# Residual graph layers with norms on one core: weights of layers 0 to 2 without output means, norms from squares on ScalarE, another order in the gate bank

## The chip, the core and the metric

The kernel runs on one core of a Trainium2 chip. The metric is the device time of one execution in microseconds (us). The core's engines are TensorE (PE in the profile, its weight loads PEld), VectorE (DVE), ScalarE (ACT), GpSimd (POOL) and SyncE (SP), which here issues the DMAs. Each works through its own queue.

## What is computed

The input x has 64 batches of 256 nodes with 128 channels, in fp32; adj is a 256 x 256 matrix shared by all batches. Four layers follow one another, each of the form `x = layernorm(x + layer(x))`, the norm running over the 128 channels:

```python
# layer 0: powers of adj, each with weights of its own (adj is given twice)
y = sum over k of (adj^k x) @ weight_1[:, :, k]
# layer 1
y = adj @ (x @ weight) + bias
# layer 2
A = adj + I;  d = rowsum(A) ** -0.5;  y = (d A d) @ x @ W.T + b
# layer 3: five steps of a gated recurrence, h = x at first
av = concat(adj @ h, adj @ h);  u3 = h @ u3_w.T + u3_b
z = sigmoid(av @ w3_w.T + w3_b + u3)
r = sigmoid(av @ w4_w.T + w4_b + u3)
hv = tanh(av @ w5_w.T + w5_b + (r * h) @ u5_w.T + u5_b)
h = (1 - z) * h + z * hv
# the norm
(x - mean(x)) / sqrt(var(x) + 1e-5)
```

## The kernel before

**Groups.** Two batches make a group, 32 groups in all; up to eight are under way at once. A group's values are tiles of 128 partitions by 512 columns: four blocks (q) of 128, each 128 nodes by 128 channels in the natural layout, so that a norm is over a block's columns.

**The order is planned.** Each operation is recorded with its engine, an estimated cost, a lag, and the values that it reads and writes (`Plan.add`). `Plan.order` then places them one by one: of all that are ready, the one that can start first, and among equals the older group. PSUM banks (eight) and SBUF slots are handed out by the same plan. The instructions are issued in this order, so the order in each engine's queue is fixed when the kernel is built, from the estimates and not from what the chip does.

**Layers 0 to 2.** Layer 0 uses w0s, which holds the weights of x (with the identity added, which gives the residual), of adj x, and of the next two powers, each the sum of both weights. It is transposed on the way through `p`, `v` and `s0`. Layers 1 and 2 propagate y (`propagate`, a product in seven block products with sums made by GpSimd and DVE, see `seven`), multiply by the weights (w1s; w2T, a transposed copy of w2) into a bank `py`, and add yb, which is y plus the bias made on GpSimd (L711). `residual` (L481) adds py and yb on DVE.

**The norm.** `statistics` takes a tile s: on DVE four bn_stats (L461), four bn_aggr (L465), var + EPS (L467) and the negated mean (L468); on GpSimd (var + EPS) ^ -0.5 (L471) and mean times that (L472). `normalise` (L489) then makes y on ScalarE, one ACTIVATE a block, with the scale and the bias given per partition. All four norms of a group go this way, 128 in all.

**Layer 3.** hT is the transposed state, brought by way of DRAM (`turned`, `brought`; between the steps `packed`). Each step propagates h into m (mg in the profile), and one bank, pr, takes u3 hT and then w4 m; ACT reads r from it (L638). w34 is w3 less w4: added to the same bank it turns r's sum into z's. A second bank, ph, takes w5 m and u5 (r h) for hv. DVE makes rh, d, e and the new hT (L645).

**Start.** SP issues the loads of adj, of the first x, of the weights and biases, then the copies aTp and w0p that are spread over partitions in another way, and further loads of x. `pre` gives each a rank. The first two groups get their transposed x through TensorE; later ones through a transposition on DVE and DRAM.

Of the kernel before, what the change touches and what calls it, by code (L numbers as in the profile page):

```python
# [9 lines left out]
AF = mybir.ActivationFunctionType  # L10
OP = mybir.AluOpType
AX = mybir.AxisListType

P = 128
# [8 lines left out]
EPS = 1e-5  # L23
# [133 lines left out]
def kernel(  # L157
# [30 lines left out]
    nc = tc.nc  # L188
    B, N, C = x.shape
# [7 lines left out]
    def mm(o, lhsT, rhs, start, stop, shared=False):  # L197
        nc.tensor.matmul(o, lhsT, rhs, start=start, stop=stop, skip_group_check=shared)  # L198
# [7 lines left out]
    def constant(name, shape):  # L206
        v = Val("const", shape, name)
        v.tile = const.tile(shape, F32, name=name)
        return v
# [4 lines left out]
    def pre(rank, engine, cost, run, reads=(), writes=()):  # L214
        lag = {"SP": 2300, "PE": 260, "DVE": 260, "ACT": 130, "POOL": 100}[engine]
        plan.add(engine, cost, lag, rank, run, reads, writes)

    def load(rank, name, shape, src, keep=True):
        v = constant(name, shape) if keep else Val("w", shape, name)
        pre(rank, "SP", 450, lambda: nc.sync.dma_start(v.ap, src), [], [v])  # L220
        return v

    ident = const.tile([P, P], F32, name="ident")
    make_identity(nc, ident)
    half = const.tile([P, Q], F32, name="half")
# [18 lines left out]
    aT, a2T = constant("aT", [P, T, N]), constant("a2T", [P, T, N])  # L244
# [30 lines left out]
    w0s = constant("w0s", [P, 4, C])  # L275
# [6 lines left out]
    pre(-7, "DVE", 1300, w0_sums, [w0_raw], [w0s])  # L282


    w0p = constant("w0p", [P, 2, C])

    def permuted():
# [15 lines left out]
    ahat, anT = Val("w", [P, T, N], "ahat"), constant("anT", [P, T, N])  # L303
# [27 lines left out]
    def block_sums(rank, name, aTs):  # L331
# [3 lines left out]
        def run():  # L335
# [13 lines left out]

    w1s = load(1.3, "w1s", [P, C], w1)
    b1s = load(1.4, "b1s", [P, C], bass.AP(tensor=b1.tensor, offset=b1.offset, ap=[[0, P], [1, C]]))
    raw = {name: load(1.5, f"raw_{name}", [P, src.shape[1]], src, False)
           for name, src in (("w2", w2), ("w4", w4_w), ("w3", w3_w), ("w5", w5_w), ("u3", u3_w), ("u5", u5_w))}
    b2s = load(1.5, "b2s", [P, C], bass.AP(tensor=b2.tensor, offset=b2.offset, ap=[[0, P], [1, C]]))
    both = {name: Val("w", [P, C], f"both_{name}") for name in ("w4", "w3", "w5", "w34")}
    for name in ("w4", "w3", "w5"):
        pre(0.4, "DVE", 220, lambda o=both[name], i=raw[name]: nc.vector.tensor_add(
# [1 line left out]
    pre(0.4, "DVE", 220, lambda: nc.vector.tensor_sub(both["w34"].ap, both["w3"].ap, both["w4"].ap),  # L361
        [both["w3"], both["w4"]], [both["w34"]])

    def transposed(name, *parts_):
        ps, v = temp(f"p_{name}"), constant(name, [P, len(parts_) * P])

        def run():
            for i, src in enumerate(parts_):
                nc.tensor.transpose(ps.ap[:, i * P:(i + 1) * P], src.ap, ident)

        n = len(parts_) * P
        pre(0.4, "PE", len(parts_) * 110, run, parts_, [ps])
        pre(0.4, "ACT", act_cost(n), lambda: nc.scalar.copy(v.ap, ps.ap[:, :n]), [ps], [v])
        return [(v, v.ap[:, i * P:(i + 1) * P]) for i in range(len(parts_))]

    w2T, u3T = transposed("w2u3T", raw["w2"], raw["u3"])
    w4T, w34T, w5T, u5T = transposed("w435u5T", both["w4"], both["w34"], both["w5"], raw["u5"])

# [11 lines left out]
    def nat(v):  # L390
        return v.ap.rearrange("p (q c) -> p q c", c=C)
# [21 lines left out]
    class Group:  # L413
# [41 lines left out]
        def statistics(self, tag, s):  # L455
            st, mv, ve, rs, nm = (self.val(k, n + tag) for k, n in (
                ("st", "st"), ("mv", "mv"), ("ve", "ve"), ("rs", "rs"), ("ve", "nm")))

            def stats():
                for q in range(self.q):  # L460
                    nc.vector.bn_stats(st.ap[:, q * 6:(q + 1) * 6], nat(s)[:, q, :])  # L461

            def aggr():
                for q in range(self.q):
                    nc.vector.bn_aggr(mv.ap[:, 2 * q:2 * q + 2], st.ap[:, q * 6:(q + 1) * 6])  # L465
                mean, var = (mv.ap.rearrange("p (q k) -> p k q", k=2)[:, k] for k in range(2))
                nc.vector.tensor_scalar(ve.ap, var, EPS, None, op0=OP.add)  # L467
                nc.vector.tensor_scalar(nm.ap, mean, -1.0, None, op0=OP.mult)  # L468

            def scales():  # L470
                nc.gpsimd.tensor_tensor(rs.ap, ve.ap, half[:, :self.q], op=OP.pow)  # L471
                nc.gpsimd.tensor_tensor(mv.ap[:, :self.q], nm.ap, rs.ap, op=OP.mult)  # L472

            self.dve(stats, [s], [st], 195 * self.q)
            self.dve(aggr, [st], [mv, ve, nm], 67 * self.q + 240)
            self.add("POOL", 1420, 100, scales, [ve, nm], [rs, mv])
            return mv, rs

        def residual(self, tag, ps, resid, left=lambda v: v.ap, right=lambda v: v.ap):
            s = self.val("w", "s" + tag)  # L480
# [152 lines left out]
        def product(self, ps, w, rhs, start, stop, shared=False):  # L633
            self.pe(pe_cost(self.width), lambda: mm(ps.ap, w[1], rhs.ap, start, stop, shared), [rhs, w[0]], [ps])

        def gate_(self, name, ps, func, bias):
            t = self.val("w", name)
            self.act(lambda: nc.scalar.activation(t.ap, ps.ap, func, bias=bias[1], scale=1.0),  # L638
                     [ps, bias[0]], [t],
                     act_cost(self.width) + 100)  # L640
            return t
# [6 lines left out]
        def record(self):  # L648
# [7 lines left out]
            else:  # L656
# [9 lines left out]
                def run():  # L666
                    f = far.ap.rearrange("(k j) (r b n) -> b (j r) k n", k=4, r=4, b=self.nb)
                    for b in range(self.nb):
                        nc.sync.dma_start(xT.ap.rearrange("p (b k n) -> b p k n", b=self.nb, k=4)[b], f[b])
# [3 lines left out]
            v, s0 = self.val("w", "v"), self.val("w", "s0")  # L673
            py = []
# [16 lines left out]
            for t in range(T):  # L691
# [9 lines left out]

                self.pe(pe_cost(self.nb * C, T), second, [v, aT], [py[t]])
                self.act(summed, [py[t]], [s0], act_cost(self.nb * C))
            y = self.normalise("0", s0, *self.statistics("0", s0))


            for tag, ats, w, bias in (("1", aT, (w1s, w1s.ap), b1s), ("2", anT, w2T, b2s)):
                yb = self.val("w", "yb" + tag)

                def biased(yb=yb, y=y, bias=bias):  # L710
                    nc.gpsimd.tensor_tensor(nat(yb), nat(y), bias.ap[:, None, :].to_broadcast([P, self.q, C]),  # L711
                                            op=OP.add)

                self.add("POOL", 40 + 625 * self.nb, 100, biased, [y, bias], [yb])
                m = self.propagate(tag, y, ats)
                py = self.val("bank", "py" + tag)

                def weight(py=py, m=m, w=w):
                    for q in range(self.q):
                        mm(py.ap[:, q * P:(q + 1) * P], m.ap[:, q * P:(q + 1) * P], w[1], True, True)  # L720

                self.pe(pe_cost(P, self.q), weight, [m, w[0]], [py])
                y = self.normalise(tag, *self.residual(tag, py, yb))


            h = y
            hT = self.brought("hT", self.turned("h", h, "p (q k j) -> p q k j", "p (k q i) -> p q k i"))
            ats, ins = aT, None
            for s in range(STEPS):
                m = self.propagate(f"g{s}", h, ats, ins, True)  # L730
                pr = self.val("bank", f"pr{s}")
                self.product(pr, u3T, hT, True, False)
                self.product(pr, w4T, m, False, True)
                r = self.gate_(f"r{s}", pr, AF.Sigmoid, rb)
                rh = self.tensor(f"rh{s}", OP.mult, r, hT)
                ph = self.val("bank", f"ph{s}")
                self.product(ph, w5T, m, True, False)
                self.product(pr, w34T, m, False, True, shared=True)
                z = self.gate_(f"z{s}", pr, AF.Sigmoid, zb)
                self.product(ph, u5T, rh, False, True)  # L740
                hv = self.gate_(f"hv{s}", ph, AF.Tanh, hb)

                d = self.tensor(f"d{s}", OP.subtract, hv, hT)
                e = self.tensor(f"e{s}", OP.mult, z, d)
                if s < STEPS - 1:
                    hT = self.tensor(f"hT{s}", OP.add, hT, e)
                    h, ats, ins = self.packed(f"h{s}", hT), aTp, pairs
            if self.start < B - END:
                hT = self.tensor("hT", OP.add, hT, e)
# [3 lines left out]
            else:  # L753
                hT = self.tensor("hT", OP.add, hT, e, lambda v: v.ap.rearrange("p (k q i) -> p q k i", k=4, q=self.q),
                                 lambda v: v.ap.rearrange("p (q k i) -> p q k i", k=4, q=self.q))
# [23 lines left out]
    with tc.manual_schedule():  # L779
        for op in plan.order():  # L780
            for v in op.vals:
                if v.tile is None:
                    pool = {"bank": psum_b, "dram1": dram, "dram2": dram}.get(v.kind, sbuf)
                    full = SHAPES.get(v.kind, v.shape)
                    t = pool.tile(full, F32, tag=f"{v.kind}{v.slot}", name=v.name)
                    if v.shape != full:
# [3 lines left out]
                        t = t[:, :n]  # L790
                        if len(v.shape) == 3:
                            t = t.rearrange("p (a b) -> p a b", b=v.shape[2])
# [32 lines left out]
```

## Time and profile before

| | |
|---|---|
| time, median of three runs | 1392.04 us (1391.99 to 1392.26) |
| time of the profiled execution | 1391.42 us |
| mean granted TensorE clock | 0.993 |
| chain that ended last | PE 82%, DVE 13%, issue 2%, ACT 2%, DMA 1%, SPq 1% |
| DMA | 134.45 MB, 97 GB/s |
| r, z and hv on ACT | 160 each, 685 ns |
| rh, d, e, hT on DVE | 160 each, 787, 766, 761 and 788 ns |
| bn_aggr; var + EPS; negated mean on DVE | 512 of 151 ns; 128 of 252; 128 of 168 |
| power; mean times scale on GpSimd | 128 of 1123 ns; 128 of 265 |

How to read it: a row of the page's groups names the line, the engine, the operation, the tiles that it writes and reads with their shapes, and how often it runs; then the busy time in us and the mean duration of one in ns; then how long the engine had been idle before such instructions, and which instruction ended most of that (the releaser). Instructions of one engine overlap in part, so that the busy time of a group can be less than its number times its mean. An fp32 product shows as two matmul records, each with a weight load. The chain that ended last is followed back from the end of the execution, at each step to what released it.

### The profile page before, as it was taken

How to read it: one execution, taken by the hardware profiler on the slowest of the kernel's cores; microseconds unless marked ns; L12 is line 12 of the kernel's file. 1: busy time of each engine (PE TensorE's matmuls, PEld its weight loads, DVE VectorE, ACT ScalarE, POOL GpSimd, SP SyncE). 2: the span in 40 equal slices, each digit the busy share in tenths (PEclk: the TensorE clock that was granted, in tenths of full speed). 3: DMA queues.
4: the chain of work that ended last, by engine and by line, in shares of the span. 5: the costliest groups of instructions: out<-in, count | busy, mean ns of one | idle time of the engine just before them, and what ended most of it. 6: DMA issues, size and time to landing. Idle time of an engine off the chain costs nothing.

```text
span 1389.6 us, 22166 instructions
## 1 busy us (share of the span) xinstructions
PE 1347.1 (97%) x6516; PEld 928.3 (67%) x6516; DVE 1114.0 (80%) x3288; ACT 691.1 (50%) x1638; POOL 754.7 (54%) x1089
## 2 busy tenths in 40 slices
PE   8999999999999999999999999999999999899996
PEld 7976656676666766666577775666766667665663
DVE  5678779788887798888778798788888777988776
ACT  3554445455454445545455554544555444554444
POOL 4776526475564474754267575636655435853332
PEclk9999999999999999999999999999999999999998
DMA  6112225333343342433433323343333332133232
GB/s 190 33 54 84 84 69 167 100 98 100 91 115 91 101 113 72 131 88 117 117 87 104 93 77 91 92 128 101 91 115 107 91 90 71 52 124 104 87 91 61
DMA packets 269672, 134.45 MB, mean 97 GB/s; under 512 B 176368, under 2 KB 241392, under 8 KB 269552
## 3 DMA queue, kind: packets, MB, share of 16 engines
q1 hardware_dynamic: 269552, 133.03, 33.0%
q8 instruction: 53, 0.87, 0.3%
q14 instruction: 67, 0.55, 0.1%
HBM read 67.05 MB, written 65.54 MB: 95 GB/s over the span
## 4 chain that ended last, share of the span: by engine, by line
PE 82%; DVE 13%; issue 2%; ACT 2%; DMA 1%; SPq 1%; DVEq 0%; POOL 0%; ACTq 0%; POOLq 0%
PE pr L198 27%; PE ph L198 18%; PE pmg L198 16%; PE py L198 13%; PE pm L198 6%; PE pmq L198 2%; DVE hT L645 2%; DVE d L645 2%; DVE e L645 2%; DVE st L461 1%; DVE s L481 1%; DMA x<-in_x_dram 1%; DVE rh L645 1%; ACT hv L638 1%; DVE th L620 1%
## 5 line engine op out<-in xcount | busy, mean ns | idle before, releaser
L198 PE MATMUL pr<-mg,w435u5T 128*128 128x512 f32 x640 | 325.0, 597 | 2.3 <-DVE mg L569 2.2
L471 POOL TENSOR_TENSOR rs<-ve,half 128x4 f32<-128x4 f32 x128 | 143.7, 1123 | 232.8 <-DVE nm L468 230.7
L531 POOL TENSOR_TENSOR tsg<-h 128x256 f32<-128x256 f32 x128 | 105.2, 822 | 253.5 <-DMA h<-dh 187.6
L489 ACT ACTIVATE y<-s,mv,rs 128x128 f32<-128x128 f32 x512 | 210.6, 483 | 44.1 <-POOL mv L472 42.7
L638 ACT ACTIVATE z<-pr,bsum 128x512 f32<-128x512 f32 x160 | 109.5, 685 | 127.2 <-PE pr L198 125.0
L645 DVE TENSOR_TENSOR rh<-r,hT 128x512 f32<-128x512 f32 x160 | 125.9, 787 | 53.7 <-ACT r L638 52.8
L198 PE MATMUL pr<-hT,w2u3T 128*128 128x512 f32 x320 | 163.4, 598 | 4.2 <-DVE hT L645 3.3
L645 DVE TENSOR_TENSOR d<-hv,hT 128x512 f32<-128x512 f32 x160 | 122.5, 766 | 55.0 <-ACT hv L638 54.2
L198 PE MATMUL ph<-rh,w435u5T 128*128 128x512 f32 x320 | 163.5, 596 | 2.0 <-DVE rh L645 1.9
L638 ACT ACTIVATE r<-pr,bsum 128x512 f32<-128x512 f32 x160 | 109.6, 685 | 109.4 <-PE pr L198 109.1
L198 PE MATMUL ph<-mg,w435u5T 128*128 128x512 f32 x320 | 163.6, 593 | 0.0
L198 PEld LDWEIGHTS pr<-mg,w435u5T 128*128 128x128 f32 x640 | 110.2, 191 | 76.9 <-issue 59.1
L638 ACT ACTIVATE hv<-ph,bsum 128x512 f32<-128x512 f32 x160 | 109.2, 685 | 48.5 <-PE ph L198 47.9
L645 DVE TENSOR_TENSOR hT<-hT,e 128x512 f32<-128x512 f32 x160 | 125.6, 788 | 1.4
L198 PEld LDWEIGHTS pmg<-aTp,h 128*128 128x128 f32 x512 | 88.6, 197 | 52.7 <-issue 38.3
L198 PEld LDWEIGHTS pmg<-s_aTp,tsg 128*128 128x128 f32 x768 | 101.8, 191 | 32.2 <-issue 26.1
L645 DVE TENSOR_TENSOR e<-z,d 128x512 f32<-128x512 f32 x160 | 121.4, 761 | 1.4
L461 DVE BATCH_NORM_STATS2 st<-s 128x6 f32<-128x128 f32 x512 | 110.5, 275 | 3.6 <-ACT s L699 3.0
L198 PE MATMUL pmg<-s_aTp,tsg 128*128 128x128 f32 x768 | 106.5, 275 | 0.2 <-POOL tsg L535 0.2
L581 ACT COPY mg<-pmg 128x128 f32<-128x128 f32 x160 | 42.3, 264 | 121.6 <-PE pmg L198 90.4
L198 PE MATMUL pmg<-aTp,h 128*128 128x128 f32 x512 | 98.7, 280 | 0.5 <-DVE mq L569 0.3
L198 PEld LDWEIGHTS ph<-mg,w435u5T 128*128 128x128 f32 x320 | 58.0, 192 | 57.4 <-issue 41.6
(159 smaller groups left out, 2686.6 us busy)
## 6 DMA issues: line engine op xcount, KB each, us to landing
dh<-th SPq DMA_DIRECT2D x160, 256.0 KB, 2.0
h<-dh SPq DMA_DIRECT2D x256, 128.0 KB, 2.5
x<-in_x_dram SPq DMA_DIRECT2D x32, 256.0 KB, 3.4
hT<-dh SPq DMA_DIRECT2D x128, 64.0 KB, 2.0
out_dram<-y SPq DMA_DIRECT2D x32, 256.0 KB, 2.4
dx<-tx SPq DMA_DIRECT2D x30, 256.0 KB, 2.6
xT<-dx SPq DMA_DIRECT2D x60, 128.0 KB, 2.6
dn<-tn SPq DMA_DIRECT2D x28, 256.0 KB, 2.0
```

Of the source, the lines that this page charges most:

```text
L198: nc.tensor.matmul(o, lhsT, rhs, start=start, stop=stop, skip_group_check=shared)
L461: nc.vector.bn_stats(st.ap[:, q * 6:(q + 1) * 6], nat(s)[:, q, :])
L471: nc.gpsimd.tensor_tensor(rs.ap, ve.ap, half[:, :self.q], op=OP.pow)
L481: self.dve(lambda: nc.vector.tensor_add(right(s), left(ps), right(resid)), [ps, resid], [s])
L489: nc.scalar.activation(nat(y)[:, q, :], nat(s)[:, q, :], AF.Identity, bias=mv.ap[:, q:q + 1], scale=rs.ap[:, q:q + 1])
L531: nc.gpsimd.tensor_tensor(ts.ap[:, :2 * P].rearrange("p (x c) -> p x c", x=2), ins(h)[:, 1], ins(h)[:, :, 0], op=OP.subtract)
L581: self.act(lambda: nc.scalar.copy(o(m, 0), o(ps, 0, False)), [ps], [m], act_cost(P), True)
L620: self.dve(lambda: nc.vector.transpose(turn.ap.rearrange("p (u j t) -> p u t j", t=T, j=32), src.ap.rearrange("p (u t i) -> p u t i", t=T, ...
L638: self.act(lambda: nc.scalar.activation(t.ap, ps.ap, func, bias=bias[1], scale=1.0), [ps, bias[0]], [t], act_cost(self.width) + 100)
L645: self.dve(lambda: nc.vector.tensor_tensor(out(t), way(a), way(b), op=op), [a, b], [t])
```

## The change

Weights and biases of layers 0 to 2 are centred: from every row of w0s, of w1, and of the two biases the mean over the output channels is taken off, on DVE, before first use; for w2 the transposition is replaced by a product with the identity less 1/128. The outputs of these layers then have mean zero over the channels, as y has. So their norms need the mean square alone: ScalarE squares each block with an accumulator output, GpSimd adds EPS and takes the power, and ScalarE multiplies by it. The norm of layer 3 stays as it was. In each step of layer 3, w4 m is now the first product in the bank pr, and u3 h the second. w1, b1 and b2 are loaded into one tile, wb, with b2 written after b1.

```diff
+    def centre(v, means):
+        nc.vector.reduce_sum(means.ap, v.ap, axis=AX.X)
+        nc.vector.tensor_scalar(means.ap, means.ap, -1.0 / C, None, op0=OP.mult)
+        nc.vector.tensor_tensor(v.ap, v.ap, means.ap[:, :, None].to_broadcast(v.ap.shape), op=OP.add)
+    w0m = constant("w0m", [P, 4])
+    pre(-7, "DVE", 1500, lambda: centre(w0s, w0m), [w0s], [w0s, w0m])
...
-    w1s = load(1.3, "w1s", [P, C], w1)
-    b1s = load(1.4, "b1s", [P, C], bass.AP(tensor=b1.tensor, offset=b1.offset, ap=[[0, P], [1, C]]))
+    wb, wbm = constant("wb", [P, 3, C]), constant("wbm", [P, 3])
+    pre(1.3, "SP", 450, lambda: nc.sync.dma_start(wb.ap[:, 0, :], w1), [], [wb])
+    for i, b in ((1, b1), (2, b2)):
+        pre(1.4, "SP", 450, lambda i=i, b=b: nc.sync.dma_start(
+            wb.ap[:, i, :], bass.AP(tensor=b.tensor, offset=b.offset, ap=[[0, P], [1, C]])), [wb], [wb])
+    pre(0.35, "DVE", 1100, lambda: centre(wb, wbm), [wb], [wb, wbm])
...
-    b2s = load(1.5, "b2s", [P, C], bass.AP(tensor=b2.tensor, offset=b2.offset, ap=[[0, P], [1, C]]))
...
+    less = constant("less", [P, P])
+    pre(0.4, "DVE", 200, lambda: nc.vector.tensor_scalar(less.ap, ident, -1.0 / C, None, op0=OP.add), [], [less])
...
-                nc.tensor.transpose(ps.ap[:, i * P:(i + 1) * P], src.ap, ident)
+                if src is raw["w2"]:
+                    mm(ps.ap[:, i * P:(i + 1) * P], src.ap, less.ap, True, True)
+                else:
+                    nc.tensor.transpose(ps.ap[:, i * P:(i + 1) * P], src.ap, ident)
...
+        def spread_of(self, tag, s):
+            y, ve, rs = self.val("w", "y" + tag), self.val("ve", "ve" + tag), self.val("rs", "rs" + tag)
+            def squares():
+                for q in range(self.q):
+                    nc.scalar.activation(nat(y)[:, q, :], nat(s)[:, q, :], AF.Square, scale=C ** -0.5,
+                                         accum_out=ve.ap[:, q:q + 1])
+            def scales():
+                nc.gpsimd.tensor_scalar(ve.ap, ve.ap, EPS, None, op0=OP.add)
+                nc.gpsimd.tensor_tensor(rs.ap, ve.ap, half[:, :self.q], op=OP.pow)
+            self.act(squares, [s], [y, ve], 400 * self.q)
+            self.add("POOL", 1330, 100, scales, [ve], [ve, rs])
+            return y, rs
+        def normalise_centred(self, tag, s):
+            y, rs = self.spread_of(tag, s)
+            def run():
+                for q in range(self.q):
+                    nc.scalar.mul(nat(y)[:, q, :], nat(s)[:, q, :], rs.ap[:, q:q + 1])
+            self.act(run, [s, rs], [y], 380 * self.q)
+            return y
+        def added(self, tag, ps, resid):
+            s = self.val("w", "s" + tag)
+            self.dve(lambda: nc.vector.tensor_add(s.ap, ps.ap, resid.ap), [ps, resid], [s])
+            return s
...
-            y = self.normalise("0", s0, *self.statistics("0", s0))
+            y = self.normalise_centred("0", s0)
...
-                y = self.normalise(tag, *self.residual(tag, py, yb))
+                y = self.normalise_centred(tag, self.added(tag, py, yb))
...
-                self.product(pr, u3T, hT, True, False)
-                self.product(pr, w4T, m, False, True)
+                self.product(pr, w4T, m, True, False)
+                self.product(pr, u3T, hT, False, True)
```

More of the change, by code (lines that the diff above doesn't have):

```diff
@@ L348 @@
     block_sums(0.7, "aTp", aTp)
-    w1s = load(1.3, "w1s", [P, C], w1)
-    b1s = load(1.4, "b1s", [P, C], bass.AP(tensor=b1.tensor, offset=b1.offset, ap=[[0, P], [1, C]]))
+    wb, wbm = constant("wb", [P, 3, C]), constant("wbm", [P, 3])
[4 more added lines that the diff above has]
+    pre(0.35, "DVE", 1100, lambda: centre(wb, wbm), [wb], [wb, wbm])
+    w1c, b1c, b2c = ((wb, wb.ap[:, i, :]) for i in range(3))
     raw = {name: load(1.5, f"raw_{name}", [P, src.shape[1]], src, False)
            for name, src in (("w2", w2), ("w4", w4_w), ("w3", w3_w), ("w5", w5_w), ("u3", u3_w), ("u5", u5_w))}
-    b2s = load(1.5, "b2s", [P, C], bass.AP(tensor=b2.tensor, offset=b2.offset, ap=[[0, P], [1, C]]))
     both = {name: Val("w", [P, C], f"both_{name}") for name in ("w4", "w3", "w5", "w34")}
@@ L368, in run @@
             for i, src in enumerate(parts_):
-                nc.tensor.transpose(ps.ap[:, i * P:(i + 1) * P], src.ap, ident)
+                if src is raw["w2"]:
+                    mm(ps.ap[:, i * P:(i + 1) * P], src.ap, less.ap, True, True)
+                else:
+                    nc.tensor.transpose(ps.ap[:, i * P:(i + 1) * P], src.ap, ident)
         n = len(parts_) * P
-        pre(0.4, "PE", len(parts_) * 110, run, parts_, [ps])
+        pre(0.4, "PE", len(parts_) * 110, run, [*parts_, less], [ps])
         pre(0.4, "ACT", act_cost(n), lambda: nc.scalar.copy(v.ap, ps.ap[:, :n]), [ps], [v])
@@ L634, in product, with gate_ @@
             self.pe(pe_cost(self.width), lambda: mm(ps.ap, w[1], rhs.ap, start, stop, shared), [rhs, w[0]], [ps])
-        def gate_(self, name, ps, func, bias):
-            t = self.val("w", name)
+        def gate_(self, name, ps, func, bias, kept=True):
+            t = self.val("w", name) if kept else ps
             self.act(lambda: nc.scalar.activation(t.ap, ps.ap, func, bias=bias[1], scale=1.0),
@@ L703, in record @@
                 self.act(summed, [py[t]], [s0], act_cost(self.nb * C))
-            y = self.normalise("0", s0, *self.statistics("0", s0))
-            for tag, ats, w, bias in (("1", aT, (w1s, w1s.ap), b1s), ("2", anT, w2T, b2s)):
+            y = self.normalise_centred("0", s0)
+            for tag, ats, w, bias in (("1", aT, w1c, b1c), ("2", anT, w2T, b2c)):
                 yb = self.val("w", "yb" + tag)
                 def biased(yb=yb, y=y, bias=bias):
-                    nc.gpsimd.tensor_tensor(nat(yb), nat(y), bias.ap[:, None, :].to_broadcast([P, self.q, C]),
+                    nc.gpsimd.tensor_tensor(nat(yb), nat(y), bias[1][:, None, :].to_broadcast([P, self.q, C]),
                                             op=OP.add)
-                self.add("POOL", 40 + 625 * self.nb, 100, biased, [y, bias], [yb])
+                self.add("POOL", 40 + 625 * self.nb, 100, biased, [y, bias[0]], [yb])
                 m = self.propagate(tag, y, ats)
```

## The prediction

> **What bounds the kernel now.** I read the page's shares first, then TensorE's waits, then the chain of waits around the worst stall, then the end of the span.
>
> ```profile
> span 1389.6 us, 22166 instructions
> PE 1347.1 (97%) x6516; PEld 928.3 (67%) x6516; DVE 1114.0 (80%) x3288; ACT 691.1 (50%) x1638; POOL 754.7 (54%) x1089
> ...
> L489 ACT ACTIVATE y<-s,mv,rs 128x128 f32<-128x128 f32 x512 | 210.6, 483 | 44.1 <-POOL mv L472 42.7
> ...
> L461 DVE BATCH_NORM_STATS2 st<-s 128x6 f32<-128x128 f32 x512 | 110.5, 275 | 3.6 <-ACT s L699 3.0
> ```
>
> A busy TensorE is not TensorE at its pace, so I count its work. In the chain, four records of a 512-wide product take 1.72 us, so a product (two records) costs 0.86; eight records 256 wide take 1.74 (0.435 a product); sixteen 128 wide take 1.81 (0.226). The groups hold 800, 396 and 2034 of these products and 56 transposes at about 0.11: 688 + 172 + 460 + 6 = 1326 us. The other 64 us of the span are: 5.8 idle in the first 40 us, 13.6 idle after 1370 us, 23.1 idle in between, and 21 in which records are drawn out. About 40 us lie in the long middle and can be won. Who causes them is in TensorE's waits from 40 to 1370 us (total, times, longest):
>
> ```profile
> PE pmg L198 <- DVE mg L565: 5.2, 8, 2.1
> PE pr L198 <- DVE hT L645: 3.3, 6, 1.2
> PE py L198 <- DVE m L569: 2.8, 2, 1.8
> PE pm L198 <- DVE m L565: 2.6, 2, 2.2
> ...
> PE pr L198 <- ACT hv L638: 0.7, 1, 0.7
> ```
>
> The whole list names 22.4 us; DVE is the releaser of 18.5, ACT of 1.8. The releasing instructions are products' combinations and gates, not the norms; but the norms stand before them in DVE's queue. The chain of waits at the stall of 1202 us shows it (start, us, piece):
>
> ```profile
> 1198.10 1.67 DVE hT L645
> 1199.77 0.78 DVE st L461 x4
> 1200.55 0.61 DVE tn L599
> 1201.16 0.17 DVE usg L559
> 1201.33 0.30 DVE mv L465 x4
> 1201.63 0.02 issue
> 1201.65 0.17 DVE ve L467
> 1201.82 0.07 DVE nm L468
> 1201.89 0.19 DVE wsg L562
> 1202.08 0.34 DVE m L569
> 1202.43 0.04 issue
> 1202.47 0.94 PE py L198 x6
> ```
>
> Of these 4.3 us before py, 1.3 are st, mv, ve and nm. The window from 1180 to 1240 us, with DVE busy 55.73 of 60, is TensorE's worst in the middle: 5.85 us idle.
>
> **What the Trainium skill says.** (1) "Perfetto Trace Analysis", section Identifying the Most-Contended Engine: matmul busy time is no good measure of headroom. The trace agrees: 1347 busy against 1326 of work. (2) "PSUM — Partial Sum Buffer", section Engine vs sequencer instructions: the queues of ScalarE, VectorE and GpSimd are strict first in, first out. The chain above agrees: m waits behind nm. (3) "ScalarE: Activation LUTs", section What ACT_TABLE_LOAD costs: 186 ns + 0.833 a column, 93 more for each per-partition pointer operand, and 93 overlap back to back. For 128 columns and two pointers that is 479 alone, 386 in a row; the trace has a mean of 483, and 210.6/512 = 411 in a row. No page prices the accumulator output of an ACTIVATE.
>
> **The change part by part.**
> *Statistics of layers 0 to 2 leave DVE.* There are 128 norms, of which 96 lose st, mv, ve and nm. The four groups are busy 110.5 + 46.7 + 32.2 + 21.5 = 210.9 us, 1.65 a norm, so 96 x 1.65 = 158 us go; DVE drops from 1114 to about 959 us (69%).
> *Squares come to ScalarE.* 96 x 4 = 384 ACTIVATEs with an accumulator. The trace shows none. Below: 0.29 each (the skill's price with one pointer, in a row), 113 us. Above: 0.41 plus some 0.2 for fetching the sum (an estimate: half an ACTIVATE), 234 us. I take 0.41, the measured neighbour: 158 us, ACT at 849 (61%). The normalising pass then carries one pointer fewer; worth 0 to 36 us (384 x 0.093, the skill's price); I take 0. The program as built has one table load on ACT, as before.
> *GpSimd* keeps two small operations a norm: an addition of EPS in place of nm x rs (0.265 each, 33.9/128). Near nothing; between -10 and +20 us on an engine with 635 us of idle time.
> *Latency of a norm.* Before: st 0.86, mv to nm 0.6, GpSimd 1.3, ACT 1.65. After: squares 1.65, GpSimd 1.3, ACT 1.65. No longer; hidden by other groups.
> *Gate bank.* Same two products. In TensorE's order, weighed with the durations above, a median of 15.3 us of work lies from u3 h's start to w4 m's start, and 1.7 us from w4 m's to u3 h's afterwards. A bank is held some 13 us less, 160 times; u3 h no longer stands in the queue ahead of its time waiting for hT (3.3 us of the list). Against it: r now comes one product, 0.86 us, later after m. Eight groups share TensorE, and a step of one needs 5 x 0.86 + 7 x 0.226 = 5.9 us of it, so a round takes some 47 us and 0.86 is hidden, except in the last group. Bounds -6 to +6 in the middle (twice the waits that name hT); I take 0, and +1 at the end.
> *Start.* The centring of w0s adds a reduction over 512 columns (deg's takes 0.69), a small scaling (0.17) and a 512-wide addition (0.79): 1.7 us; that of w1, b1, b2 1.4; less 0.2. The first product with w0s starts at 14.4, w0s is complete at 8.9: hidden. One transpose becomes a product: +0.1 us of TensorE. On SP no DMA is added, but the order moves: six bias loads (1.45 + 1.92 us of issue) and b1 go ahead of aTp, w0p and the third load of x, which started at 14.50 and moves to about 18.4; the fourth from 18.44 to about 18.9. The later loads of x follow at +0.4 to +3.5. TensorE lost 2.4 us to x before 27 us, and the chain runs through a load of x until 32.9, so this reaches it: +1 (0 to +3).
>
> **The sum.** What freeing DVE is worth in the 40 us has two ends. Low: DVE's share of named waits, 18.5/22.4, gives 33 us, and 14% of DVE's work goes: 4.6. High: all that st, mv, ve and nm hold of the whole chain of waits, 18.9 + 7.4 + 6.7 + 2.2 = 35 us by adding its pieces, times 96/128: 26. I take 14, a little under the middle, since the next releaser is often close behind. ScalarE's share of the waits (8% of 40 = 3.2 us for 691 busy) grows with 158 us more, and squares stand four in a row ahead of gates: +3. Net -14 + 3 + 1 + 1 = -9 against the span of 1389.6. The profiled execution took 1391.42 and the timed runs 1391.99 to 1392.26, so the span is some 2 us short of a time; the same -9 from 1392.0 gives **1383 us**.
>
> **Rivals.**
> *ScalarE takes DVE's place (slower).* Place: a square block ahead of r in ACT's queue. From the second gate product to the product with rh, TensorE's order holds a median of 3.26 us of other work, while r (0.69) and rh (0.79) need 1.5: slack 1.8. A block of four at 0.41 (1.65) just fits; at 0.6 (2.4, with the accumulator's fetch) it overruns by 0.6 to 0.9, and the order was planned with 0.4 each. If a third of the 96 blocks hit a gate at 0.9: +29, less 14, plus 2: +17, **1409**. It decides from about 0.5 us a square. For it: the accumulator is unpriced. Against it: ACT would still be 40% idle, and 1.8 of 22.4 us of waits name it.
> *More is freed than DVE's time.* Banks held 13 us less let the planner start other products earlier, and a queue at 69% instead of 80% waits far less than in proportion: the 26 us are reached and only the start's 1 is lost: **1367**. For it: the releasers' list; against it: no wait of the list names a bank clearly.
> *Hidden anyway.* TensorE is saturated and its waits move from one DVE instruction to the next (d, e and hT alone hold 70 us of the chain): low end 4.6 less the costs of 5: **1391**. That the work is not removed can be left out: the built program has 128 BNStats instructions in place of 512.
>
> **How the numbers follow.** Forecast 0.50 (1375 to 1390), more freed 0.20, hidden 0.13, ScalarE 0.17. The range 1366 to 1400 leaves out part of the second and most of the last. About 0.2% (2.8 us) is what can be told from no change: faster takes the forecast but 0.02, the second case, and 0.03 of the third: 0.71; same 0.08; slower 0.21, ScalarE and the rest of the hidden case.
>
> **What would show it.** Right: BATCH_NORM_STATS2 x128, DVE near 960 us, ACT near 850, TensorE's idle time between 40 and 1370 us down from 23 to some 13, DVE's part of its waits down most. Wrong: squares over 0.5 us in a row, or r, hv or usg of ACT at the head of TensorE's waits (ScalarE); a TensorE idle time in the middle still near 23 (hidden); more than 3 us lost before 40 us or after 1370.

## The result, and the profile after

The changed kernel takes 1368.28 us (median of four runs, 1367.05 to 1369.0) against 1392.15 before (its median with a fourth run): a ratio of 0.9827, with a 95% interval of 0.981 to 0.9844. It is 24 us faster. The prediction said 9, and its rival "more is freed" named 1367. The runs below show that neither had the reason: over six orders of each kernel the means lie 7.5 us apart, with an interval of about -1 to 16, and the rest of the 24 us goes with the order that the planner happened to make.

The page after, its shares and the rows of the norms:

```profile
span 1365.1 us, 21963 instructions
PE 1335.7 (98%) x6517; PEld 923.9 (68%) x6517; DVE 983.1 (72%) x2335; ACT 763.7 (56%) x2406; POOL 747.0 (55%) x1089
...
L521 ACT ACTIVATE y<-s,rs 128x128 f32<-128x128 f32 x384 | 122.2, 393 | 13.7 <-POOL rs L510 13.3
L505 ACT ACTIVATE y<-s 128x128 f32<-128x128 f32 x384 | 113.8, 302 | 25.5 <-DVE s L528 25.3
```

DVE lost 131 us and ScalarE gained 73. The statistics on DVE are down to layer 3's:

```profile
L505 ACT ACTIVATION_READ_ACCUMULATOR y<-s 128x1 f32 x384 | 73.5, 191 | 0.0
...
L481 DVE BATCH_NORM_STATS2 st<-s 128x6 f32<-128x128 f32 x128 | 27.5, 277 | 0.3
```

The accumulator has a second instruction for each square, 191 ns long. The timeline of ScalarE (start, length, instruction) shows that it opens no gap in a row: the squares start 0.29 to 0.31 us apart, and each fetch lies half under its own square and half under the next.

```profile
600.21 0.31 ACT L505 ACTIVATE y<-s 128x128 f32<-128x128 f32 x1 [0.24 <-DVE s L528]
600.42 0.19 ACT L505 ACTIVATION_READ_ACCUMULATOR y<-s 128x1 f32 x1
600.52 0.29 ACT L505 ACTIVATE y<-s 128x128 f32<-128x128 f32 x1
600.72 0.19 ACT L505 ACTIVATION_READ_ACCUMULATOR y<-s 128x1 f32 x1
600.81 0.29 ACT L505 ACTIVATE y<-s 128x128 f32<-128x128 f32 x1
```

So four squares follow one another in 1.18 us: 0.295 a square, the lowest of the prices that the prediction weighed. The scaling in a row takes 0.318 (122.2/384) in place of 0.411.

Where the 24.5 us of span went: TensorE's idle time between 40 and 1340 us fell from 23.1 to 9.65 (1300 less 1290.35 busy), that of the first 40 us rose from 5.8 to 6.8, that after 1340 us went from 13.6 to 13.0, and its busy time fell by 11.4. TensorE's waits from 40 to 1340 us, the first rows:

```profile
PE pmg L198 <- ACT usg L624: 2.1, 3, 1.0
PE py L198 <- DVE m L621: 1.1, 3, 0.4
PE pmg L198 <- ACT s L752: 0.9, 1, 0.9
PE pr L198 <- ACT r L691: 0.9, 2, 0.6
```

In this list DVE as releaser is down from 18.5 to 3.5 us, and ScalarE is up from 1.8 to 5.6. Idle times of 1 us and more before one matmul were five, together 9.2 us; now there is one, of 1.0. The window from 1180 to 1240 us, worst before with 5.85 idle, has 0.40:

```profile
1180.00:1240.00 60.00, 59.60 (x270) 37.34 (x269) 48.29 (x109) 32.46 (x93) 27.89 (x42) 1.00 0.38 115
```

In the chain that ended last, DVE's share went from 13% to 5% and TensorE's from 82% to 89%. The middle reads as the prediction had it, only stronger. Whether it is the change's doing is another question.

### The profile page after: what moved, and what is told of

The parts are those of the page before. It is cut to its first block, busy times and chain, and to the rows that moved or that the text cites. A ratio compares the mean times of both kernels' runs of the same rounds, so it can differ in the third digit from the quotient of the medians.

```text
span 1365.1 us, 21963 instructions
## 1 busy us (share of the span) xinstructions
PE 1335.7 (98%) x6517; PEld 923.9 (68%) x6517; DVE 983.1 (72%) x2335; ACT 763.7 (56%) x2406; POOL 747.0 (55%) x1089
## 4 chain that ended last, share of the span: by engine, by line
PE 89%; DVE 5%; DMA 2%; ACT 1%; issue 1%; POOL 1%; SPq 1%; ACTq 0%; POOLq 0%; DVEq 0%
PE pr L198 28%; PE ph L198 19%; PE pmg L198 18%; PE py L198 15%; PE pm L198 6%; PE pmq L198 3%; DMA x<-in_x_dram 1%; DVE hT L698 1%; DVE d L698 1%; DVE e L698 0%; DMA w_raw<-in_L_gnn_weight_dram 0%; DVE th L672 0%; DVE rh L698 0%; DVE st L481 0%; DMA wb<-in_L_gnn_b_dram 0%
## 5 line engine op out<-in xcount | busy, mean ns | idle before, releaser
L698 DVE TENSOR_TENSOR d<-hv,hT 128x512 f32<-128x512 f32 x160 | 118.1, 738 | 69.5 <-ACT hv L691 68.5
L198 PEld LDWEIGHTS pr<-mg,w435u5T 128*128 128x128 f32 x640 | 107.1, 191 | 56.2 <-issue 38.2
L521 ACT ACTIVATE y<-s,rs 128x128 f32<-128x128 f32 x384 | 122.2, 393 | 13.7 <-POOL rs L510 13.3
L505 ACT ACTIVATE y<-s 128x128 f32<-128x128 f32 x384 | 113.8, 302 | 25.5 <-DVE s L528 25.3
L621 DVE TENSOR_TENSOR mg<-pmg,usg 128x256 f32<-128x256 f32 x160 | 67.1, 419 | 62.8 <-PE pmg L198 59.5
L510 POOL TENSOR_TENSOR rs<-ve,half 128x4 f32<-128x4 f32 x96 | 101.9, 1062 | 8.0
L509 POOL TENSOR_SCALAR ve<-ve 128x4 f32<-128x4 f32 x96 | 24.5, 255 | 141.8 <-ACT y L505 141.8
```

What stands on the lines that cost most here:

```text
L505: nc.scalar.activation(nat(y)[:, q, :], nat(s)[:, q, :], AF.Square, scale=C ** -0.5, accum_out=ve.ap[:, q:q + 1])
L509: nc.gpsimd.tensor_scalar(ve.ap, ve.ap, EPS, None, op0=OP.add)
L521: nc.scalar.mul(nat(y)[:, q, :], nat(s)[:, q, :], rs.ap[:, q:q + 1])
L621: nc.vector.tensor_tensor(o(m, slice(1, 3)), o(ps, slice(1, 3), False), both, op=OP.add)
L698: self.dve(lambda: nc.vector.tensor_tensor(out(t), way(a), way(b), op=op), [a, b], [t])
```

## The experiments

Each runs on the same chip as runs of the kernel before, whose medians lay between 1390.98 and 1392.36 us. In the first four, theory A says that the norms' leaving DVE brings the gain, theory B that the gate bank's order does, theory C that both do.

**One edit at a time.** The first has the changed norms with the old order of the gate products, the second the new order with the old norms.

```diff
 # e1: the changed kernel
-                self.product(pr, w4T, m, True, False)
-                self.product(pr, u3T, hT, False, True)
+                self.product(pr, u3T, hT, True, False)
+                self.product(pr, w4T, m, False, True)
 # e2: the kernel before, with the two lines exchanged the other way
```

> The changed kernel with u3 h first in the gate bank again, as before; all else as changed. Theory A (the norms' leaving DVE brings the gain): 1370 to 1374 us, DVE near 983 us, TensorE idle between 40 and 1350 us near 11. Theory B (the gate bank's order brings it): 1384 to 1390. Theory C (each brings about half): 1378 to 1382.

> The kernel before with only the two gate products exchanged (w4 m, then u3 h); norms as before on DVE. Theory A: 1388 to 1393 us. Theory B: 1370 to 1376. Theory C: 1378 to 1384.

Norms only took 1378.37 us (ratio 0.9906, 0.9891 to 0.9921), 12.6 less than before; the gate order only 1381.79 (0.9937, 0.9919 to 0.9955), 9.2 less. By the letter that is theory C, and the two sum to 21.8, near the whole. It would have been a neat end.

**Is it the time for which the bank is held?** In the next, u3 h comes first again, but is recorded as reading m too, so that the bank is opened only then.

```diff
-                self.product(pr, w4T, m, True, False)
-                self.product(pr, u3T, hT, False, True)
+                self.pe(pe_cost(self.width), lambda pr=pr, hT=hT: mm(pr.ap, u3T[1], hT.ap, True, False),
+                        [hT, m, u3T[0]], [pr])
+                self.product(pr, w4T, m, False, True)
```

> The changed kernel with u3 h first in the gate bank, but recorded as waiting for m too, so that the bank is opened only when m is there. If the gain of the gate edit lies in the time that the bank is held and in where u3 h stands in TensorE's queue: as the changed kernel, 1366 to 1371 us. If it lies in which product comes first: as the kernel with u3 h first and early. If Theory A holds alone, it and both others lie within 4 us of each other.

It took 1384.06 us (0.995, 0.9934 to 0.9967). In TensorE's order the median of the work from one gate product's start to the other's is 1.7 us, as in the changed kernel, and yet it is 16 us slower: the account by the bank fails as it was put. By the order of the products it should have matched the kernel with u3 h early, and it is 6 us slower than that. So something else may move these times by several us.

**The work given back to DVE, and taken off again without touching any order.** The fourth kernel does the old statistics on DVE once more, for nobody. The fifth plans them in the same way but issues nothing for them, so that TensorE's, ScalarE's and GpSimd's order is the fourth's to the last instruction.

```diff
 # e4: the changed kernel; stats and aggr as before the change, into tiles of their own
         def normalise_centred(self, tag, s):
+            self.idle_statistics(tag, s)
 # e5: the same plan
-            self.dve(stats, [s], [st], 195 * self.q)
-            self.dve(aggr, [st], [mv, ve, nm], 67 * self.q + 240)
+            self.dve(lambda: None, [s], [st], 195 * self.q)
+            self.dve(lambda: None, [st], [mv, ve, nm], 67 * self.q + 240)
```

> The changed kernel with the old bn_stats, bn_aggr and the two small operations still done on DVE for the norms of layers 0 to 2, their results read by nobody (extra work, nothing left out): DVE gets back some 158 us of busy time, ScalarE keeps the squares. Theory A: 1386 to 1394 us, DVE near 1140 busy. Theory B: 1369 to 1374. Theory C: 1378 to 1384.

> As the changed kernel with the statistics kept on DVE, and planned with them, but they are not issued (they were extra work, so nothing is left out): TensorE's, ScalarE's and GpSimd's order is that of the kernel with statistics kept, instruction for instruction, and only DVE's queue is shorter. Theory Q (a shorter DVE queue itself releases TensorE): 1376 to 1386 us against 1407 with the statistics issued. Theory P (the order of the plan decides, the queue's length little): 1396 to 1407.

With the statistics kept: 1406.93 us (1.0116, 1.0096 to 1.0137), above every theory's figure. Without issuing them, in the same order: 1392.22 (1.0004, 0.9997 to 1.0011), outside theory Q's range and theory P's alike, between the two. The engines' shares, with the statistics and without:

```profile
PE 1354.1 (96%) x6517; PEld 931.8 (66%) x6517; DVE 1106.1 (79%) x3295; ACT 766.4 (55%) x2406; POOL 739.2 (53%) x1089
PE 1351.8 (97%) x6517; PEld 932.4 (67%) x6517; DVE 984.2 (71%) x2335; ACT 766.4 (55%) x2406; POOL 742.2 (53%) x1089
```

So 122 us less on DVE brought 14.7 us, 0.12 for each, with every order the same. (The two ran on different chips; each set against the kernel before on its own chip, they differ by 16 us, 0.13 for each.) In TensorE's waits from 40 to 1340 us, those that DVE ends fall from 19.4 to 9.2 us, and those that ScalarE ends stay (8.6 and 9.0). The first rows, with the statistics kept:

```profile
PE pmg L198 <- DVE mg L635: 11.1, 12, 3.3
PE pmg L198 <- ACT usg L642: 4.6, 8, 1.9
PE pm L198 <- DVE m L635: 2.3, 2, 1.3
```

The same view of the kernel that does not issue them:

```profile
PE pmg L198 <- DVE mg L635: 6.9, 9, 2.4
PE pmg L198 <- ACT usg L642: 4.6, 8, 1.9
```

But this kernel does exactly what the changed one does, on the same engines, and is 24 us slower than it. Only the plan differs: the order, and the buffers that it hands out.

**The same work in other orders.** The planner's estimate for a DVE operation has a factor of 1.06. Moving it by 0.5 to 2% changes no work, but the plan made from it is another: with the changed kernel at 1.06 and at 1.05, fewer than one in five of TensorE's 3286 places hold the same product.

```diff
 def dve_cost(elements):
-    return (elements / 0.96 + 75) * 1.06
+    return (elements / 0.96 + 75) * 1.05
 # the other kernels: 1.07, 1.055, 1.065, 1.04
```

> The kernel before with the planner's estimate for DVE operations lowered by 1% (factor 1.06 to 1.05): the same work in another order. It measures what a redrawn order alone is worth. Theory P: 4 to 15 us away from 1391, either way. Theory Q: within 4 us of 1391.

> The changed kernel with the planner's estimate for DVE operations lowered by 1%: the same work in another order. Theory P: 4 to 15 us away from 1368, more likely above, as a single good draw returns to the mean. Theory Q: within 4 us of 1368.

> The kernel before with the planner's DVE estimate raised by 1% (1.06 to 1.07): another draw of the order. 1380 to 1395 us if draws lie some 6 us apart as the first suggests.

> The changed kernel with the planner's DVE estimate raised by 1%: another draw. If 1368 is typical and 1387 was the odd one: 1363 to 1374 us. If 1368 was a lucky draw: 1376 to 1390.

> The kernel before, planner's DVE factor 1.055. If draws of before scatter about their mean so far: 1379 to 1393 us. If 1391 is typical of before: 1388 to 1393.

> The changed kernel, planner's DVE factor 1.055. Change worth 24 us: 1364 to 1372. Change worth 9 to 12, the rest the draw: anywhere from 1367 to 1388.

> The kernel before, planner's DVE factor 1.065: as for 1.055, 1379 to 1393 us.

> The changed kernel, planner's DVE factor 1.065: as for 1.055; change worth 24: 1364 to 1372, worth 9 to 12: 1367 to 1388 us.

> The kernel before, planner's DVE factor 1.04: 1379 to 1391 us, near 1384 by the mean of its draws.

> The changed kernel, planner's DVE factor 1.04. Change worth 24: 1364 to 1372; worth some 7, the rest the draw: 1367 to 1388, near 1377 by the mean of its draws.

| factor | before, us | TensorE idle 40 to 1340 us | changed, us | TensorE idle 40 to 1340 us |
|---|---|---|---|---|
| 1.06 (as given) | 1392.15 | 23.1 | 1368.28 | 9.7 |
| 1.05 | 1385.67 | 19.4 | 1387.18 | 21.1 |
| 1.07 | 1380.60 | 16.7 | 1375.24 | 14.4 |
| 1.055 | 1384.77 | 18.9 | 1370.92 | 11.3 |
| 1.065 | 1378.77 | 13.2 | 1385.13 | 17.3 |
| 1.04 | 1390.58 | 21.2 | 1380.91 | 13.4 |
| mean (standard deviation) | 1385.4 (5.3) | | 1377.9 (7.7) | |

The means differ by 7.5 us, with a standard error of 3.8 (the root of 5.3²/6 + 7.7²/6), so roughly -1 to 16 as a 95% interval: a gain is likely, but not shown beyond doubt. The kernel before, as given, is the slowest of its six; the changed one is the fastest of its six. Without these two, the five redraws have means of 1384.1 and 1379.9, only 4.2 apart. Of the ten expectations, those that took 24 us for the change's worth held in one of four (1.055), and three results lay outside every range given: 1387.18, 1375.24 and, narrowly, 1378.77. In the pairs of the same factor the difference runs from 24 us faster to 6 slower. The time goes with TensorE's idle time: from the order with the least to that with the most, 9.9 us more idle stand against 13.4 us of time before, 11.4 against 18.9 after.

What an unlucky order looks like, in the timeline of the changed kernel at 1.05 (three of its eight idle times over 1 us; in brackets the idle time and the releaser):

```profile
188.78 0.69 PE L198 MATMUL pmg<-s_aTp,h 128*128 128x128 f32 x2 [2.58 <-issue]
...
234.80 0.38 PE L198 MATMUL pmg<-aTp,h 128*128 128x128 f32 x1 [2.74 <-ACT usg L624]
...
1024.08 0.50 PE L198 MATMUL pmg<-s_aTp,h 128*128 128x128 f32 x2 [1.66 <-DVE mg L617]
```

Over the six orders of each kernel, such idle times are 30 before and 24 after. DVE releases 22 of the 30 before, but 10 of the 24 after, where ScalarE releases 11. By all waits in this stretch it is the same: those that DVE ends fall from a mean of 12.1 us to 5.8, and those that ScalarE ends rise from 3.9 to 6.6. The norms' move thus shows in who is waited for, in all orders together.

**The two prices, in the orders as given.** One kernel is that of before, in its own order, with the statistics of layers 0 to 2 left out on DVE. The other is the changed one, in its own order, with one 4-column square for the four of 128 columns.

```diff
 # e9: before, for layers 0 to 2
+            if tag != "3":
+                def stats():
+                    nc.vector.memset(st.ap, 0.0)
+                def aggr():
+                    nc.vector.memset(ve.ap, 1.0)
+                    nc.vector.memset(nm.ap, 0.0)
 # e10: changed
-                for q in range(self.q):
-                    nc.scalar.activation(nat(y)[:, q, :], nat(s)[:, q, :], AF.Square, scale=C ** -0.5,
-                                         accum_out=ve.ap[:, q:q + 1])
+                nc.scalar.activation(ve.ap, nat(s)[:, 0, :self.q], AF.Square, scale=C ** -0.5)
```

> The kernel before in its own order, with the statistics of layers 0 to 2 left out on DVE: three small memsets stand for bn_stats, bn_aggr and the two small operations, so the norms of these layers scale by 1 and nothing is centred (this part of the computation is left out). GpSimd's and ScalarE's work stays. If a shorter DVE queue is worth the same 14 to 15 us as in the other order: 1375 to 1380 us. If it depends on the order: 1380 to 1388, or under 1372.

> The changed kernel in its own order, with one 4-column square in place of the four 128-column squares with accumulator (the mean squares of layers 0 to 2 are left out, their norms scale by something else). What it gains over 1368 is what the squares cost there. The prediction's +3: 1364 to 1366 us. If squares cost nothing: 1367 to 1369. If they stand in the way of the gates: under 1360.

The shares without the statistics, and without the squares:

```profile
PE 1342.7 (98%) x6516; PEld 927.4 (67%) x6516; DVE 996.8 (72%) x2616; ACT 691.0 (50%) x1638; POOL 747.7 (54%) x1089
PE 1337.6 (98%) x6517; PEld 925.6 (68%) x6517; DVE 980.7 (72%) x2335; ACT 667.0 (49%) x1734; POOL 749.8 (55%) x1089
```

Without the statistics: 1379.22 us (0.9917, 0.9901 to 0.9934), 12.0 less than the 1391.23 of before beside it. DVE's busy time fell from 1114.0 to 996.8, since the memsets stay, so that is 0.10 us for each us of DVE; in the other order it was 0.12. Without the squares: 1368.34 us, against 1368.28 with them; ScalarE's busy time fell from 763.7 to 667.0. In this order, 97 us of ScalarE cost nothing that can be measured.

The first of these kernels also tests the chain of waits that the prediction read at 1202 us. TensorE's order is that of before, and the wait ahead of the same product is gone (before, then without the statistics):

```profile
1202.47 0.94 PE L198 MATMUL py<-w1s,m 128*128 128x128 f32 x6 [1.81 <-DVE m L569]
1189.20 1.09 PE L198 MATMUL py<-w1s,m 128*128 128x128 f32 x8
```

Of the other waits over 1 us, that of 2.07 falls to 1.04 and that of 1.18 to 0.48; those of 1.94 and 2.18 stay.

**Truer estimates.** The planner counts 400 ns for a square and 380 for a scaling; the profile after has 295 and 318.

```diff
-            self.act(squares, [s], [y, ve], 400 * self.q)
+            self.act(squares, [s], [y, ve], 300 * self.q)
-            self.act(run, [s, rs], [y], 380 * self.q)
+            self.act(run, [s, rs], [y], 320 * self.q)
```

> The changed kernel with the planner's costs of the squares and of the scaling on ScalarE set near what the profile after shows (a square 0.295 us in a row and a scaling 0.318: estimates 300 and 320 in place of 400 and 380). If true costs help the plan: 1362 to 1367 us. If any new order is a new draw: 1364 to 1380.

1364.32 us (0.98, 0.9785 to 0.9814), the fastest of all and 4 us below the changed kernel. It is worth keeping as a kernel. As a rule it shows nothing: it lies in both ranges, and one order that lies 4 us off, where orders scatter by 7.7, may be one more draw. Counted with the kernel that plans the statistics and does not issue them (1392.22), it gives eight orders of the changed work: their mean stays at 1378.0, and their standard deviation is 9.9.

## Why the prediction was wrong

**Which step failed.** The sum, by a term that it lacks. It set "-14 + 3 + 1 + 1 = -9 against the span of 1389.6", as if the rest of the order stayed as it was, and gave the redrawn order no term at all. The plan is made anew from end to end whenever an operation goes or comes; a change of 0.5 to 2% in one estimate, with no work changed, is worth up to 13 us before (1391 to 1379) and 19 us after (1368 to 1387). The 24 us divide, by the six orders of each, into 7.5 between the means, 6.7 by which the kernel before stood above its own mean, and 9.7 by which the changed one stands below its. The range of 1366 to 1400 held the time, but its ends came from other causes, and that the rival "more is freed" named a figure within 2 us is luck: the mean of the changed kernel's six orders is 1378.

**Freeing DVE, taken as -14.** About right where the order is held, though not by the sum that led to it. The 158 us were the busy times of four groups added up, but instructions of DVE overlap: the same statistics, issued or not, moved DVE's busy time by 122 us, and in the changed kernel it fell by 131. At 0.10 to 0.13 us for each us, found in two orders that were held fixed, these 131 us are worth 13 to 17. The low end, 4.6 by proportion, is too low there; the high end, 26 by the chain's pieces, was not reached. What the same load is worth once the plan is redrawn is not shown.

**ScalarE, taken as +3.** Nothing, where it was tried. The squares take 0.295 us and not 0.41, the fetch of the sum opens no gap between squares, and the scaling saves the 36 us that I had left at 0. So ScalarE gained 73 us where I had 158. The slower rival decided from 0.5 us a square and fell with that. Still, over the six orders ScalarE takes DVE's place as the releaser of 11 of 24 long waits, and the waits that it ends grow by 2.7 us. So in a redrawn plan the +3 may hold; no run priced the squares there.

**The gate bank, taken as 0.** Not settled. The new order of the two products alone took 1381.79 us, well inside the range that the kernel before covers by redrawing (1378.77 to 1392.15). Norms only, at 1378.37, lies inside the changed kernel's. That 12.6 and 9.2 add up to about the 24 is therefore no proof for either part. That the bank's shorter hold helps, the ground of the faster rival, is not borne out, nor is it refuted: with the bank held as short, the kernel with u3 h late took 1384.06, but that is one order too. A fixed order could not be used here, since this edit is itself a change of order.

**Start, +1, and end, +1.** The first 40 us have 1.0 more idle, as put. After 1340 us there is 0.6 less; the last group's later r did not show.

**The reading of the bottleneck.** Right for the order as given: its waits lie in DVE's queue, and the changed kernel won 13.5 of idle time in the middle and 11.4 of drawn-out work. The stall at 1202 us was indeed the statistics' to remove: in the same order, without them, it is gone. What the trace of one order could not show is that this was also that order's stall: another order of the same kernel (1.065) has 10 us less idle in the middle with all its norms on DVE.

What is left open: the change's own worth, within about -1 to 16 us, and how the 7.5 divides between the norms, for which the fixed orders say 12 or more, and the rest.

## What to carry to other kernels

Where a planner or a scheduler fixes the order, an edit is compared with one draw of the order against another. Redraw both sides several times (six of each left 3.8 us of standard error here), by a change in an estimate that touches no work, before the difference is put on the edit. To price a load by itself, keep the plan and issue nothing for it: then the other engines' order is the same, and the difference is the load's.

## What the runs showed of the hardware

An idle time on TensorE can be paid twice. The kernel before waits 2.07 us for mg, until 325.28 us. Its stretches of 1 us around that (length; busy time and instructions of PE, PEld, DVE, ACT and POOL; then the granted clock, the DMA share, GB/s):

```profile
324.00:325.00 1.00, 0.00 (x0) 0.00 (x0) 0.97 (x9) 0.00 (x0) 0.55 (x1) 1.00 0.61 236
325.00:326.00 1.00, 0.72 (x6) 0.72 (x7) 1.00 (x7) 0.22 (x1) 0.67 (x2) 1.00 0.07 27
326.00:327.00 1.00, 1.00 (x8) 1.00 (x7) 0.87 (x4) 1.00 (x4) 0.77 (x2) 0.56 0.18 54
327.00:328.00 1.00, 1.00 (x4) 0.62 (x3) 0.76 (x4) 0.57 (x3) 0.88 (x2) 0.50 0.52 147
328.00:329.00 1.00, 1.00 (x3) 0.34 (x2) 0.57 (x1) 0.00 (x0) 0.90 (x2) 0.50 0.21 62
329.00:330.00 1.00, 1.00 (x3) 0.52 (x2) 0.04 (x1) 0.69 (x1) 0.92 (x3) 0.73 0.53 209
330.00:331.00 1.00, 1.00 (x8) 0.86 (x7) 0.73 (x1) 0.00 (x0) 0.18 (x1) 1.00 0.14 53
```

Some 0.8 us after work resumes the clock falls to half for about 3.4 us, which loses 1.7 us more (0.44 + 0.50 + 0.50 + 0.27), while TensorE reads as fully busy. The same follows the 1.81 us wait at 1202 us. The waits of 1.94 us at 193 and of 2.18 us at 514 have no such sequel. Yet the wait of 2.18 us for the same product has one in the kernel without the statistics, whose TensorE order is the same (before, then without):

```profile
514.15 0.46 PE L198 MATMUL pm<-s_anT,y 128*128 128x128 f32 x2 [2.18 <-DVE m L565]
507.52 0.55 PE L198 MATMUL pm<-s_anT,y 128*128 128x128 f32 x2 [2.18 <-DVE m L573]
```

So the length of a wait doesn't decide alone; where it falls does too. The clock records of the trace before have the two low stretches start at 326.12 and 1203.35 us, 877.23 apart, which is 257.0 times 3.413. If a grid of this step is laid through the whole trace (an inference from these starts), the waits of 2.07 and 1.81 us lie whole in the step just ahead of a low stretch, while the others are cut: the step with most of the 2.18 has 1.88 us idle, that of the 1.94 has 1.40. In the kernel without the statistics the 2.18 us lie whole in one step, ahead of the low stretch that starts at 507.76. Other traces agree on the grid (the changed kernel at 1.05: starts at 188.87 and 356.12, 49.0 steps apart); the idle time from which a step counts is not settled, since 1.81 had a sequel and 1.88 had none.

The changed kernel has no such stretch between 40 and 1350 us: the 3.4 us lost before are part of the 11.4 by which busy time fell; the other 8 were not traced. Idle time and the half clock behind it make up most of the scatter of the orders. From 40 to 1340 us the six of the kernel before, in the order of the table, have 2, 2, 1, 0, 0 and 3 steps at half clock, those of the changed kernel 0, 3, 1, 0, 4 and 2. If TensorE's idle time from 40 to 1340 us and 1.7 us for each of these steps are taken off, the six orders of the kernel before lie between 1362.2 and 1365.9 us, and those of the changed kernel between 1358.6 and 1364.1.

The Trainium skill, "TensorE: Matmul & The Clock Gate", Part 1, has the clock fall to half after an idle window of about 3.4 us; the traces here show it after pauses of about 2, with a low stretch of the length that the page names.
